# Cutting the stores of one chunk by rows into unequal pieces

## The chip, the cores and the metric

The kernel runs on one core of one Trainium2 chip. The engines are called by their usual names: TensorE, VectorE, ScalarE (ACT), GpSimd and SyncE (SP). The profile counts sixteen DMA engines; here they move data between HBM and the tiles of 128 partitions in the on-chip memory (SBUF). A "row" below is one partition's share of a store: 6 x 1024 floats, 24,576 bytes, for the wide chunks. Every transfer in the traces names a semaphore, and its landing is recorded as updates of that semaphore, called "landing marks" below. Each of the eight stores of chunk 14 left sixteen marks in the trace of before; with sixteen engines in the profile, one mark is read as one engine.

## The reference, cut to what matters

```
emb = emb_table.at[0].set(0.0)            # 100001 x 128
e = emb[seq]                              # 1024 x 50 x 128
uF = cumsum(e, axis=1) / min(t, length)
y = batch_norm(uF)                        # over the 1024 sequences
...                                       # 50 spiking steps: v += (x - v) / 2; spike where v >= 1
uF_out = spikes.mean(axis=0)              # 1024 x 128
scores = uF_out @ emb.T                   # 1024 x 100001 floats: 410 MB
```

The last line is what this case is about: 410 MB must be written.

## The kernel before

The first stage gathers embeddings and runs the 50 steps. The second multiplies the spike counts with the table and stores the scores. Its columns come in chunks, `WIDTHS` giving their width in parts of 1024 columns; each chunk has eight blocks of 128 output rows. A block is collected in one of three buffers `o` and leaves in one store.

```python
WIDTHS = [2, 2, 2, 3, 3, 3, 3] + 12 * [6] + [4, 4]
...
    def store(n, c0, o):
        nc.sync.dma_start(out=out[n * P : (n + 1) * P, c0 : c0 + o.shape[1]], in_=o)
...
    for c, W in enumerate(WIDTHS):
        ...
                turns = [(rowp, "rows2", 6), (rowp, "rows3", 6), (op, "o", 6)]     # c >= 7
        ...
        for n in range(NB):                                                        # NB = 8
            pool, tag, most = turns[blocks % len(turns)]
            o = pool.tile([P, most * HALF], F32, tag=tag, name=f"o_{c}_{n}")
            for q in range(q0, q1):
                ...                                        # products into PSUM, copied to o
            if c or n > 1:
                store(n, q0 * HALF, o[:, : min(N, q1 * HALF) - q0 * HALF])
            ...
            if n in (1, 4) and c >= MIDDLE and to_fetch < parts:
                ...
                fetch(r, to_fetch, GROUP // 2)             # 1.5 MB of table, issued from ACT
```

## Time and profile before

| | before |
|---|---|
| median of the runs | 1576.41 us |
| profiled execution: span | 1646.4 us |
| profiled execution: first store to end | 1064.3 us |
| stores of 3 MB | 96, 20.3 us to landing |
| DMA share and GB/s, 60 us from the start of chunk 14 | 1.00, 416 |

One caution for reading the traces. The stage before the first store takes about 511 us in some executions and about 585 us in others, with the same program. The profiled execution of before is one of the long ones, which is why its span is 70 us above the median.

From the first store on the executions agree: up to chunk 14, where all kernels of this case are alike, the fourteen traces took 638.5 to 639.9 us. So I compare traces by this second stage, and runs only with the runs of before on the same chip in the same rounds.

### The profile page before, as it was taken

The page shows a single profiled execution, that of the slowest core. Times are in us where ns is not written, and L with a number is a line of the kernel's source. Part 1 is how long each engine was busy: PE and PEld are TensorE (multiplying, and loading weights), DVE is VectorE, ACT ScalarE, POOL GpSimd, SP SyncE. Part 2 cuts the span into 40 slices and gives each one's busy share as a digit, 9 for nine tenths or more (in the row PEclk, how much of TensorE's full clock was granted, in tenths as well). Part 3 has the DMA queues.
Part 4 walks back from the last instruction along what each step waited for, and adds up shares of the span by engine and source line. Part 5 has one row for each costly group of instructions (what it writes and reads, how often), then busy time and mean ns, then how long its engine had stood idle before and what let it go on. Part 6 is the DMA issues. An engine that isn't in the chain of part 4 may idle for free.

```text
span 1646.4 us, 12555 instructions
## 1 busy us (share of the span) xinstructions
PE 1115.2 (68%) x4538; PEld 829.4 (50%) x4548; DVE 940.4 (57%) x1161; ACT 630.6 (38%) x700; POOL 379.3 (23%) x406
## 2 busy tenths in 40 slices
PE   4344433444334498889987888888888888788885
PEld 2122211222113276667766666666666666666664
DVE  4566655666556766557655555555555555555553
ACT  2222222222222255446544444444444444444442
POOL 7666666666666500000000000000000000000000
PEclk9999999999755599999999999999999999999998
DMA  9511111111111179999999999999999999999898
GB/s 342 213 45 48 47 48 43 47 48 48 48 43 49 39 320 412 416 422 398 426 422 429 432 428 427 421 420 429 420 423 412 415 421 421 428 425 423 381 428 350
DMA packets 53691, 488.14 MB, mean 296 GB/s; under 512 B 11995, under 2 KB 12796, under 8 KB 32380
## 3 DMA queue, kind: packets, MB, share of 16 engines
q1 hardware_dynamic: 31984, 428.77, 62.0%
q0 software_dynamic: 12800, 26.24, 5.5%
q10 hardware_dynamic: 8844, 32.33, 5.0%
q8 instruction: 36, 0.59, 0.1%
q14 instruction: 27, 0.22, 0.0%
HBM read 77.69 MB, written 409.60 MB: 296 GB/s over the span
## 4 chain that ended last, share of the span: by engine, by line
DMA 48%; DVE 22%; another core or an unknown queue 10%; PE 9%; ACT 5%; issue 4%; POOL 1%; DVEq 0%; ACTq 0%; SPq 0%
DMA scores<-o 48%; PE po L149 8%; ACT o L456 4%; DVE bs L306 4%; DVE uF L305 4%; DVE v L342 3%; DVE s L326 3%; DVE negv L348 3%; DVE o L454 2%; POOL e L187 1%; DVE a L335 1%; DVE mv L316 1%; DVE q L332 0%; PE pt L119 0%
## 5 line engine op out<-in xcount | busy, mean ns | idle before, releaser
L454 DVE TENSOR_SCALAR o<-po 128x1024 f32<-128x1024 f32 x391 | 463.7, 1221 | 352.4 <-DMA scores<-o 326.9
L456 ACT ACTIVATE o<-po 128x1024 f32<-128x1024 f32 (+1 forms) x391 | 388.0, 1019 | 548.2 <-DMA scores<-o 345.0
L187 POOL DMA_INDIRECT e<-in_L_rec_emb_table,idx x400 | 378.6, 947 | 188.8 <-issue 109.8
L149 PE MATMUL po<-pairs,countB 128*128 128x512 f32 x1168 | 313.9, 415 | 66.8 <-ACT o L456 49.6
L149 PEld LDWEIGHTS po<-pairs,countB 128*128 128x128 f32 x1168 | 225.4, 198 | 131.3 <-ACT o L456 64.4
L149 PE MATMUL po<-pairs,countC 128*128 128x512 f32 x876 | 238.2, 417 | 43.2 <-ACT o L456 43.0
L253 PE MATMUL pre<-zT,l 128*128 128x512 f32 x100 | 74.6, 748 | 247.2 <-DVE uF L305 159.5
L149 PEld LDWEIGHTS po<-pairs,countC 128*128 128x128 f32 x876 | 168.8, 199 | 89.3 <-ACT o L456 54.8
L253 PEld LDWEIGHTS pre<-zT,l 128*128 128x128 f32 x100 | 27.7, 279 | 286.9 <-issue 183.0
L305 DVE SCALAR_TENSOR_TENSOR uF<-rlen,pre 128x512 f32<-128x512 f32 x100 | 68.0, 680 | 180.5 <-remote 145.0
L320 ACT ACTIVATE r<-mv,eps 128x1 f32<-128x1 f32 x50 | 14.7, 295 | 378.8 <-DVE mv L316 269.4
L142 DVE TENSOR_TENSOR pairs<-pt,pairs 128x1024 fp32r<-128x1024 f32 (+1 forms) x73 | 88.4, 1217 | 94.7 <-ACT pairs L141 94.7
L296 PE MATMUL pre<-ident,e 128*128 128x128 f32 x400 | 107.2, 426 | 25.8 <-DMA e<-in_L_rec_emb_table,idx 17.7
L119 PE MATMUL pt<-ident,rows 128*128 128x128 f32 x782 | 113.1, 292 | 8.3 <-ACT o L456 3.7
L119 PEld LDWEIGHTS pt<-ident,rows 128*128 128x128 f32 x782 | 102.3, 154 | 28.6 <-issue 9.8
L296 PEld LDWEIGHTS pre<-ident,e 128*128 128x128 f32 x400 | 85.3, 223 | 60.9 <-DMA e<-in_L_rec_emb_table,idx 32.2
L149 PE MATMUL po<-hi,countB 128*128 128x512 f32 x200 | 82.9, 414 | 19.2 <-ACT o L456 14.9
L264 PE MATMUL sums<-s,ident_h 128*128 128x512 bf16 x88 | 45.3, 606 | 64.2 <-DVE s L326 32.8
L149 PE MATMUL po<-lo,countB 128*128 128x512 f32 x200 | 80.4, 402 | 0.0
L149 PE MATMUL po<-pairs,countA 128*128 128x512 f32 (+1 forms) x292 | 73.5, 393 | 9.1 <-ACT o L456 9.1
L141 ACT CAST pairs<-pt 128x1024 fp32r<-128x1024 f32 (+1 forms) x73 | 73.6, 1008 | 15.0 <-PE pt L119 14.9
L149 PE MATMUL po<-hi,countC 128*128 128x512 f32 x150 | 63.2, 421 | 17.7 <-ACT o L456 17.7
(76 smaller groups left out, 849.8 us busy)
## 6 DMA issues: line engine op xcount, KB each, us to landing
scores<-o SPq DMA_DIRECT2D x96, 3072.0 KB, 20.3
scores<-o SPq DMA_DIRECT2D x32, 1536.0 KB, 9.0
rows<-in_L_rec_emb_table ACTq DMA_DIRECT2D x20, 1536.0 KB, 29.2
scores<-o SPq DMA_DIRECT2D x22, 1024.0 KB, 8.6
rows<-in_L_rec_emb_table SPq DMA_DIRECT2D x6, 3072.0 KB, 42.7
scores<-o SPq DMA_DIRECT2D x8, 2048.0 KB, 13.2
scores<-o SPq DMA_DIRECT2D x8, 1872.5 KB, 11.3
e<-in_L_rec_emb_table,idx POOLq DMA_INDIRECT x400
```

The source lines that it names most:

```text
L119: nc.tensor.transpose(pt[:, k0 : k0 + kw], r[:kw, k0 : k0 + D], ident[:kw, :kw])
L141: nc.scalar.copy(vh, vp)
L142: nc.vector.tensor_tensor(vl, vp, vh.bitcast(F32), ALU.subtract)
L149: nc.tensor.matmul(po[:, :kw], lhsT=counts[n], rhs=part[:, k0 : k0 + kw], start=j == 0, stop=j == 1,)
L187: nc.gpsimd.indirect_dma_start(out=es[t][:, n * P : (n + 1) * P], out_offset=None, in_=table, in_offset=bass.IndirectOffsetOnAxis(ap=idx[: ...
L253: nc.tensor.matmul(pre[h], lhsT=l, rhs=zT[:, h * BANK : (h + 1) * BANK], start=t == 0, stop=False, skip_group_check=True,)
L296: nc.tensor.matmul(pre[h][:, k : k + P], lhsT=e[:, h * BANK + k : h * BANK + k + P], rhs=ident, start=False, stop=last, is_transpose=True, ...
L305: nc.vector.scalar_tensor_tensor(uF[:, cs], rlen[:, cs], 1.0 / (t + 1), pre[h], ALU.max, ALU.mult)
L306: nc.vector.bn_stats(bs[:, h, :], uF[:, cs])
L326: nc.vector.tensor_single_scalar(s, v, V_TH, ALU.is_ge)
L454: nc.vector.tensor_scalar_mul(o[:, h0 : h0 + hw], po[:, :hw], 1.0 / T)
L456: nc.scalar.mul(o[:, h0 : h0 + hw], po[:, :hw], 1.0 / T)
```

## The change

It leaves bytes, arithmetic and buffers alone. The eight stores of chunk 14 become transfers of unequal numbers of rows, and two stores of the last chunk become 120 and 8 rows.

```diff
+UNEVEN = 14
+PIECES = [(1, 7, 120), (2, 6, 120), (3, 5, 120), (4, 4, 120), (40, 88), (24, 104), (56, 72), (9, 15, 104)]
...
-    def store(n, c0, o):
-        nc.sync.dma_start(out=out[n * P : (n + 1) * P, c0 : c0 + o.shape[1]], in_=o)
+    def store(n, c0, o, pieces=(P,)):
+        b = 0
+        for rows_of in pieces:
+            nc.sync.dma_start(
+                out=out[n * P + b : n * P + b + rows_of, c0 : c0 + o.shape[1]],
+                in_=o[b : b + rows_of, :],
+            )
+            b += rows_of
+        assert b == P
...
-                store(n, q0 * HALF, o[:, : min(N, q1 * HALF) - q0 * HALF])
+                pieces = (P,)
+                if c == UNEVEN:
+                    pieces = PIECES[n]
+                elif c == len(WIDTHS) - 1 and n % 4 == 3:
+                    pieces = (120, 8)
+                store(n, q0 * HALF, o[:, : min(N, q1 * HALF) - q0 * HALF], pieces)
```

## The prediction

Three things to know for this text and for the expectations:

- "Ports" and "port conflicts" name an assumption: DMA engines that read certain partitions at once hold each other up. "Full step" is its worst case, in which every row concerned takes two row times of 912 ns. The packet records name no engine.
- That one engine is in every piece was assumed too. With 10 + 10 + 10 + 10 + 12 + 10 + 10 + 10 rows it would have 82 where it had 64: 18 more, 16.4 us at 912 ns, an estimate.
- "Eight semaphores in turn" is in the records: in the trace of before the issues of SyncE name eight, 25 or 26 transfers to each if the loads of ScalarE, which use the same ones, are counted too. The store issued at 1548.0 us names the same one as the load issued at 1501.9 us, whose last mark came 46.0 us after issue. The gathers from GpSimd name eight others.

> **What bounds the kernel now.** I read the forty slices first, then the chain of waits, the issues of transfers, and the windows around the stores that change. The slices show two stages. Up to about 580 us the sixteen DMA engines are a tenth busy; from then on they are at 9 tenths in every slice, moving 400 to 430 GB/s, almost to the end:
>
> ```profile
> DMA  9511111111111179999999999999999999999898
> GB/s 342 213 45 48 47 48 43 47 48 48 48 43 49 39 320 412 416 422 398 426 422 429 432 428 427 421 420 429 420 423 412 415 421 421 428 425 423 381 428 350
> ...
> DMA scores<-o 48%; PE po L149 8%; ACT o L456 4%; DVE bs L306 4%; DVE uF L305 4%; DVE v L342 3%; DVE s L326 3%; DVE negv L348 3%; DVE o L454 2%; POOL e L187 1%; DVE a L335 1%; DVE mv L316 1%; DVE q L332 0%; PE pt L119 0%
> ...
> scores<-o SPq DMA_DIRECT2D x96, 3072.0 KB, 20.3
> ```
>
> The chain of waits is stores for 48% of the span. The 96 stores of 3 MB (twelve chunks of eight blocks) land 20.3 us after issue. Chunk 14's eight are issued from 1225.6 to 1288.3 us. The chain in order of time shows the rhythm there, for every third store: about 20 us of landing, about 4 us to refill the freed buffer.
>
> ```profile
> 1251.03 20.67 DMA scores<-o
> 1272.88 2.13 PE po L149 x8
> 1276.09 20.32 DMA scores<-o
> 1297.58 2.13 PE po L149 x8
> 1300.79 20.94 DMA scores<-o
> ```
>
> Three buffers go round, so one store is issued per 25/3 = 8.4 us. When a store is issued the two before it are mostly still queued, so a late issue is cheap. The windows confirm that the engines never lack work there, and show the single place where they do:
>
> ```profile
> 1180.00:1250.00 70.00, 56.91 (x249) 44.42 (x248) 37.01 (x32) 29.41 (x31) 0.00 (x0) 0.94 1.00 418
> 1250.00:1320.00 70.00, 59.93 (x262) 47.67 (x261) 36.78 (x31) 31.67 (x32) 0.00 (x0) 0.92 0.99 417
> ...
> 1540.00:1550.00 10.00, 8.08 (x36) 6.37 (x35) 4.60 (x4) 4.00 (x4) 0.00 (x0) 1.00 0.62 262
> ...
> SPq L158 <- DMA rows<-in_L_rec_emb_table: 13.4, 1, 13.4
> ```
>
> The last two columns of the windows are the DMA share and GB/s; TensorE is busy 60 of 70 us and not the bound. The last line is SyncE's one long wait for a load: transfers of the hardware queues use eight semaphores in turn, and one store had to wait for a slow load that held its semaphore.
>
> Two readings go below the views, to the trace's own records of packets and landings. A 24,576-byte row is one packet, of 912 ns in the median. Each DMA engine leaves its own landing mark, and these show that the sixteen are not equal: of the store issued at 1276.1 us the eighth or ninth engine finishes 12.8 us after issue, the fifteenth 15.1, the last 20.3. **One straggler engine is some 6 us (six to seven rows) behind the rest, and it alone paces the stores.** Its lag grows by about 0.9 us per 35 us after 786 us, which fits the instruction-fetch packets (36 of 16 KB, about 0.95 us each, one per 35 us) all going to it.
>
> [...]the 33-row load left eleven engines' marks. The slowest of these came at 1551.8 us, when only the straggler still had store rows[...].
>
> [...]a 1.5 MB load (24 packets of 4 KB per engine) takes 29.2 us among store rows, and 24 x (0.912 + 0.159) = 26 us.
>
> **The change part by part.** No byte, no arithmetic and no buffer changes. Eight stores become twenty in chunk 14, and two of the last chunk become four.
>
> Issue: fourteen more at 0.332 us, on SyncE, which mostly waits. Nothing on the path.
>
> Engine loads[...], in rows: 128 rows are 8 on each engine, 64 for the chunk. Pieces of 1, 7 and 120 use 1, 7 and 15 engines (1, 1 and 8 rows each); 40 and 88 use 10 and 11 (4 and 8); 24 and 104, 12 and 13 (2 and 8); 56 and 72, 14 and 12 (4 and 6); 9, 15 and 104, 9, 15 and 13 (1, 1 and 8). [...]The part is worth 10 to 17 us.
>
> Last chunk: 120 + 8 rows put 9 rows[...] instead of 8, twice; a row of 14,980 bytes takes 0.57 us, so 1.1 us. **Without port conflicts the sum is 11 to 18 us: about 1590.**
>
> Ports: I assume that a piece is cut into runs of neighbouring partitions[...]. Most engines land within 0.5 us of each other, so they stay in step, [...]I take 40 to 70 us, centre 58. **With port conflicts: about 1635.**
>
> **The rivals.** First, counts alone (1587 to 1595). For it: the profile shows no port conflict[...]. [...]Second, conflicts (1616 to 1652); reversed arguments. Third, the wait moves to SyncE: with two to three transfers per store, eight semaphores cover only three stores, some 25 us, less than the 29 us of a load, so the second piece of the fifth store may wait about 4 us for the load issued after the second. Two stores are queued then, so the engines should not starve: 0 to 4 us. [...]Nothing makes the kernel faster, because the path's engine gains rows in every case I find likely.
>
> **Range and chances.** [...]I give conflicts 58%[...]. The mixture is 0.42 x 1590 + 0.58 x 1635 = 1616. I predict 1618 us, range 1586 to 1652. Slower by over 2% begins at 1607.9, which is past the first outcome and short of the second: 0.57 slower, 0.42 the same, 0.01 faster.
>
> **What would show it.** Look at chunk 14, from about 1225 us. The store records should show 20 issues, with the loss all there and the rhythm before and after unchanged. If counts alone hold, packets of 24,576 bytes stay at 912 ns, DMA share falls to about 64/82 of before, 0.78, in that window, and it grows by 10 to 17 us. If conflicts hold, many packets there take about 1.8 us, the busy share stays high while GB/s falls towards 250 to 300, and the window nearly doubles. A long wait of SyncE for a landing with idle engines would show the third rival.[...]

## More of the kernel before

The metric is device microseconds of one execution; medians are over the fast runs.

The following line, from the view of the tile `scores` of the kernel before, gives the first and the last issue of a store (582.1 and 1634.3 us from the start):

```profile
L158 SPq DMA_DIRECT2D scores<-o x172: 332/332/361, 582.1 to 1634.3; - x172
```

## The result, and the profile after

| | before | after |
|---|---|---|
| median of 4 runs | 1576.41 us | 1634.72 us |
| first store to end, profiled | 1064.3 us | 1121.3 us |
| chunk 14: its first copy into `o` to that of chunk 15 | 67.7 us | 103.3 us |
| from there to the first copy of chunk 20 | 309.7 us | 324.0 us |
| from there to the end | 47.7 us | 55.4 us |

The kernel became 3.7% slower, by 58.3 us: ratio 1.0369, 95% interval 1.0351 to 1.0387. (Ratios are the mean time of one kernel's fast runs over that of the other's in the same rounds, so not quite the ratio of the medians.) The three lower rows are taken from the start times of the copies in the two traces. Up to chunk 14 the two are alike (639.2 and 638.5 us from the first store). Chunk 14 loses 35.6 us until its last block starts to be followed by chunk 15, another 14.3 us shows in the next chunks, mostly while chunk 14's last stores land, and the last chunk loses 7.7 us.

The same line of the tile `scores` after:

```profile
L163 SPq DMA_DIRECT2D scores<-o x187: 236/332/3836, 511.4 to 1617.6; - x187
```

Store number one comes at 511.4 us here, so chunk 14 starts about 1151 us in this trace and about 1222 us in the one of before. The forty slices of the kernel after have a hole there, which those of before have not, in GB/s but hardly in the DMA share:

```profile
DMA  9622222222224999999999999999987899999898
GB/s 341 227 53 52 54 53 52 53 53 53 52 54 187 417 411 421 398 421 425 429 428 431 426 428 413 421 421 428 324 281 211 338 402 422 428 429 425 380 422 297
```

Windows of 60 us from the start of chunk 14 say it in one line each. The columns are the window, its length, busy time with number of instructions for TensorE, its weight loads, VectorE, ScalarE and GpSimd, then granted clock, DMA share and GB/s. First the kernel before, then after:

```profile
1222.00:1282.00 60.00, 47.25 (x209) 37.18 (x210) 30.33 (x27) 26.25 (x28) 0.00 (x0) 0.94 1.00 416
```

```profile
1151.00:1211.00 60.00, 41.83 (x171) 32.82 (x170) 24.68 (x22) 20.81 (x21) 0.00 (x0) 0.86 0.95 298
```

The engines are nearly as busy as before (0.95 against 1.00) and move 298 GB/s where they moved 416. So in this window they are hardly short of work: their packets are slow. The packet records agree. In 120 us from the start of chunk 14, 34% of the 24,576-byte packets take over 1.5 us, in the kernel before 1%; half of all still take up to 949 ns.

The chain of waits of the kernel after, in order of time, has the same rhythm as before until 1136 us, then landings of 29 to 40 us, then the rhythm again:

```profile
1136.43 20.68 DMA scores<-o
...
1163.63 28.93 DMA scores<-o
...
1199.31 30.09 DMA scores<-o
...
1233.09 39.78 DMA scores<-o
...
1278.91 25.20 DMA scores<-o
...
1308.49 20.70 DMA scores<-o
```

And there is a new wait. SyncE waited three times for a load, once for 28.8 us, in the middle of chunk 14 (stores were issued at 1199.3 and next at 1230.6 us); before, it was one wait of 13.4 us, near the end of the program:

```profile
SPq L163 <- DMA rows<-in_L_rec_emb_table: 50.7, 3, 28.8
```

Towards the end of this wait, with nothing issued, the engines do run dry, as two windows of the kernel after show:

```profile
1215.00:1225.00 10.00, 7.93 (x32) 6.32 (x32) 3.58 (x3) 3.98 (x4) 0.00 (x0) 0.66 0.63 210
1225.00:1235.00 10.00, 4.43 (x11) 3.47 (x11) 4.62 (x4) 2.53 (x3) 0.00 (x0) 0.69 0.47 115
```

That makes three suspects: more rows on some engines than on others ("counts"), engines that hold each other up by the partitions they read at once ("conflicts", in the texts on record "ports"), and waiting for a semaphore that a load holds ("semaphores": the store issued at 1230.6 us names the one of the load issued at 1199.4, whose last mark came at 1230.5). The experiments part them.

### The profile page after: what moved, and what is told of

It is laid out like the page before. It is cut to its first block, busy times and chain, and to the rows that moved or that the text cites. A ratio compares the mean times of both kernels' runs of the same rounds, so it can differ in the third digit from the quotient of the medians.

```text
span 1632.6 us, 12593 instructions
## 1 busy us (share of the span) xinstructions
PE 1170.1 (72%) x4548; PEld 834.7 (51%) x4548; DVE 942.1 (58%) x1161; ACT 631.6 (39%) x700; POOL 378.3 (23%) x406
## 4 chain that ended last, share of the span: by engine, by line
DMA 53%; POOL 17%; PE 11%; issue 9%; ACT 5%; DVE 3%; SPq 0%; ACTq 0%; DVEq 0%; POOLq 0%
DMA scores<-o 46%; POOL e L197 17%; PE po L152 10%; ACT o L466 4%; DMA e<-in_L_rec_emb_table,idx 4%; DMA rows<-in_L_rec_emb_table 3%; DVE o L464 2%; PE pt L122 0%; ACT pairs L144 0%; PE pre L306 0%; SPq L163 0%; DVE bs L316 0%; DVE pairs L145 0%; DVE uF L315 0%; DVE s L336 0%
## 5 line engine op out<-in xcount | busy, mean ns | idle before, releaser
L152 PE MATMUL po<-pairs,countB 128*128 128x512 f32 x1168 | 320.6, 421 | 83.9 <-ACT o L466 66.2
L152 PEld LDWEIGHTS po<-pairs,countB 128*128 128x128 f32 x1168 | 230.5, 202 | 150.0 <-ACT o L466 80.9
L152 PE MATMUL po<-pairs,countC 128*128 128x512 f32 x876 | 245.7, 427 | 60.1 <-ACT o L466 59.5
L306 PE MATMUL pre<-ident,e 128*128 128x128 f32 x400 | 155.6, 451 | 150.1 <-DMA e<-in_L_rec_emb_table,idx 148.7
L152 PEld LDWEIGHTS po<-pairs,countC 128*128 128x128 f32 x876 | 174.0, 205 | 107.5 <-ACT o L466 71.3
L306 PEld LDWEIGHTS pre<-ident,e 128*128 128x128 f32 x400 | 79.0, 200 | 245.4 <-DMA e<-in_L_rec_emb_table,idx 223.2
L274 PE MATMUL sums<-s,ident_h 128*128 128x512 bf16 x98 | 49.6, 609 | 61.0 <-DVE s L336 61.0
L349 ACT ACTIVATE v<-uF,hgb,a 128x1024 f32<-128x1024 f32 x49 | 59.2, 1208 | 37.5 <-DVE a L345 37.3
```

The lines of the kernel that those rows point to most:

```text
L152: nc.tensor.matmul(po[:, :kw], lhsT=counts[n], rhs=part[:, k0 : k0 + kw], start=j == 0, stop=j == 1,)
L274: nc.tensor.matmul(sums[h], lhsT=ident_h, rhs=s[:, h * BANK : (h + 1) * BANK], start=t == 0, stop=t == T - 2, skip_group_check=True,)
L306: nc.tensor.matmul(pre[h][:, k : k + P], lhsT=e[:, h * BANK + k : h * BANK + k + P], rhs=ident, start=False, stop=last, is_transpose=True, ...
L349: nc.scalar.activation(vt, uF[:, cs], AF.Identity, bias=hgb[:, 1:2], scale=a)
```

## The experiments

Two jobs landed on other chips, where the kernel before takes 1652.19 and 1648.95 us; in those profiles the stage before the first store takes 583 to 587 us, and the stage of the stores is as long as elsewhere up to chunk 14 (639 to 640 us). The column "loss" is the difference of the two medians of the same rounds. "Slow" is the share of 24,576-byte packets that took over 1.5 us, in 120 us from the start of chunk 14; a shift of that window by 1 us changes it by up to a point.

| run | before | this | loss, us | ratio | slow |
|---|---|---|---|---|---|
| the change | 1576.41 | 1634.72 | 58.3 | 1.0369 | 34% |
| chunk 14 alone | 1652.19 | 1703.05 | 50.9 | 1.0313 | 33% |
| halves, 64 + 64 | 1652.19 | 1690.70 | 38.5 | 1.0241 | 47% |
| cut by columns | 1652.19 | 1653.93 | 1.7 | 1.0012 | 1% |
| the change, loads from GpSimd | 1652.19 | 1708.41 | 56.2 | 1.0333 | 29% |
| before, loads from GpSimd | 1576.27 | 1576.97 | 0.7 | 1.0005 | 0% |
| 18 extra rows on one engine | 1576.27 | 1582.76 | 6.5 | 1.0048 | 1% |
| 120 + 8, eight times | 1576.27 | 1624.61 | 48.3 | 1.0305 | 39% |
| last chunk alone | 1576.27 | 1587.82 | 11.5 | 1.0073 | 1% |
| middle 64 twice (wrong result) | 1648.95 | 1649.86 | 0.9 | 1.0009 | 1% |
| 32 + 64 + 32 | 1648.95 | 1679.48 | 30.5 | 1.0193 | 23% |
| quarters, in order | 1648.95 | 1700.71 | 51.8 | 1.0338 | 56% |
| quarters, alternating | 1648.95 | 1672.28 | 23.3 | 1.0165 | 17% |

The 95% intervals of the ratios mean 1 to 4 us either way, but some 6 us for the change with loads from GpSimd and 7 us for 32 + 64 + 32, whose four runs spread over 12 us. A check from inside: the time from the first store to the end of each profile, less the 1064.3 us of before, agrees with the loss within 2.5 us in every run but the change with loads from GpSimd (61.7 us; its profiled run was the slowest of its four).

The absolute times in the texts on record are meant for a chip with before at 1576; the difference is what to compare.

**Chunk 14 alone.** The last chunk's stores are whole again.

```diff
-                elif c == len(WIDTHS) - 1 and n % 4 == 3:
-                    pieces = (120, 8)
```

> The changed kernel with the pieces of chunk 14 alone; the two stores of the last chunk are whole again. My term for the last chunk was 1.1 us, which would give 1633.6. If those two stores also meet a wait for a semaphore or ports in step, as the 4 to 5 us lost after chunk 14 in the trace suggest, 1629 to 1631. Either way the chunk keeps over 50 us.

The loss is 50.9 us, below the 53 to 57 of the expectation, so by difference (across two chips) the last chunk costs 7.4 us, well over the term of 1.1.

**Halves.** As above, and equal halves in chunk 14.

```diff
-PIECES = [(1, 7, 120), (2, 6, 120), ... (9, 15, 104)]
+PIECES = 8 * [(64, 64)]
```

> Chunk 14's eight stores as 64 and 64 rows: every engine keeps 4 + 4 = 8 rows, so no imbalance[...]. Theory ports: 8 rows take up to 16 row times, 8 x 7.3 us less a lead of 6, so about 1620 to 1635, and most 24,576-byte packets of the chunk take about 1.8 us. Theory counts (only rows per engine matter): 1576 to 1579, packets stay at 912 ns. Theory semaphores (SyncE waits for a load): 16 transfers in the chunk, at most one wait of a few us, 1576 to 1585.

The loss is 38.5 us with a cut that was meant to leave eight rows on every engine, and the engines were busy (0.94 in the window below), so unequal counts are not needed for most of the loss. The window of this run shows the same picture as the change, a high DMA share and few bytes:

```profile
1226.00:1286.00 60.00, 40.40 (x158) 31.70 (x159) 24.15 (x21) 19.40 (x21) 0.00 (x0) 0.86 0.94 274
```

It is below the 44 us that I expected at least, and 47% of the packets are slow, not most; why not more, the runs do not show.

**Cut by columns.** The same number of transfers per block as in the change, each of 128 rows.

```diff
-                store(n, q0 * HALF, o[:, : min(N, q1 * HALF) - q0 * HALF], pieces)
+                many = PIECES[n] if c == UNEVEN else 1      # PIECES = [3, 3, 3, 3, 2, 2, 2, 3]
+                cols = (min(N, q1 * HALF) - q0 * HALF) // many
+                for j in range(many):
+                    store(n, q0 * HALF + j * cols, o[:, j * cols : (j + 1) * cols], pieces)
```

> Chunk 14's stores cut by columns into as many transfers as in the changed kernel (3,3,3,3,2,2,2,3), each of 128 rows: equal engines, [...]only the number of transfers on the eight semaphores is the same. Theory semaphores: SyncE waits 20 us or more for a load again, 1595 to 1610. Theory ports and theory counts: 1576 to 1581; a short wait for a load may show but is hidden by the queue.

The loss is 1.7 us. SyncE waits for loads here too, three times and 38.9 us together, but the longest is 13.9 us and the engines keep their speed. (The 1% in the table counts neighbouring chunks only, since the packets of chunk 14 are smaller here; these too are quick, 312 ns in the median for 8,192 bytes and 460 for 12,288.)

```profile
SPq L163 <- DMA rows<-in_L_rec_emb_table: 38.9, 3, 13.9
```

```profile
1227.00:1287.00 60.00, 48.59 (x202) 38.23 (x202) 29.75 (x25) 25.42 (x26) 0.00 (x0) 0.89 0.99 409
```

The number of transfers as such costs next to nothing.

**Loads from GpSimd, in the change and in the kernel before.** By the records of before, transfers issued from GpSimd name semaphores that no store names (eight against eight others), so no store should have to wait for a load.

```diff
-        engine = nc.sync if q < AHEAD * GROUP else nc.scalar
+        engine = nc.sync if q < AHEAD * GROUP else nc.gpsimd
```

> The changed kernel with the later table loads issued from GpSimd, whose transfers use other semaphores, so that no store can wait for a load by sharing one. Theory ports: the 28.8 us wait of SyncE vanishes, but the engines were mostly busy with slow packets during it, so 5 to 20 us come back: 1612 to 1630. Theory semaphores: nearly all comes back: 1585 to 1600. Theory counts: 1590 to 1600.

> The kernel before with the later table loads issued from GpSimd: the base for the run with the changed kernel's loads moved, which was 56 us over the kernel before although the wait of SyncE had gone. If moving the loads costs nothing by itself, 0 to -4 us against the kernel before, and the 28.8 us wait was worth nothing. If it costs 10 us or more, the wait was worth that much after all.

In the changed kernel SyncE no longer waits for any load, and the loss is still 56.2 us. In the kernel before the move costs 0.7 us. By the medians the 28.8 us wait was worth 58.3 - (56.2 - 0.7) = 2.8 us, a difference across two chips and smaller than its noise. The traces are sharper: from the first copy of chunk 14 to that of chunk 20, the change lost 49.9 us against before, and with the loads moved in both kernels it lost 51.2. The wait cost nothing there. I had expected 5 to 20 us back: a miss. The wait looks terrible in the view of waits and in the windows, yet it lies beside engines that were late anyway: the 88-row piece issued just before it, at 1199.3 us, left its last mark at 1229.4, one us before the wait ended. While some engines ran dry (DMA share 0.63 and 0.47), others still worked off rows of that piece: three of its marks came 29.1 to 30.1 us after issue.

**18 extra rows on one engine.** The kernel before, with 18 one-row stores of partition 0 to a scratch tensor among the stores of chunk 14.

```diff
+EXTRA = [2, 2, 2, 2, 4, 2, 2, 2]
+                if c == UNEVEN:
+                    for j in range(EXTRA[n]):
+                        nc.sync.dma_start(out=scratch[sum(EXTRA[:n]) + j : sum(EXTRA[:n]) + j + 1, :], in_=o[0:1, :])
```

> The kernel before with 18 extra one-row stores of partition 0 to a scratch tensor among chunk 14's stores (2, 2, 2, 2, 4, 2, 2, 2): one engine gets exactly the 18 rows[...]. Theory counts as I predicted it: 10 us if that engine leads the straggler by 6 us, 16.6 us if it is the straggler; packets stay at 912 ns. Theory ports alone: 0 to 3 us.

6.5 us, where 18 rows take 18 x 0.912 = 16.4 us: if one engine carries them all, as assumed, about 10 us of them vanish in its lead over the straggler. The packets keep their 912 ns; the DMA share falls instead (0.86), which fits engines that wait for one. This is what counts alone look like, and it is not what the changed kernel shows:

```profile
1151.00:1211.00 60.00, 45.41 (x208) 35.84 (x208) 28.68 (x25) 24.59 (x25) 0.00 (x0) 0.95 0.86 357
```

**120 + 8, eight times.**

```diff
+PIECES = 8 * [(120, 8)]
```

> All eight stores of chunk 14 as 120 and 8 rows. By counts only one row more[...] per store: 8 rows, 7.4 us less a lead of 6, so 1 to 8 us. [...]Anything from 30 to 60 is for ports.

48.3 us, for conflicts, with 39% of the packets slow. This one cut brings nearly the loss of the eight different cuts of the change (50.9).

**The last chunk alone.**

```diff
-                if c == UNEVEN:
-                    pieces = PIECES[n]
-                elif c == len(WIDTHS) - 1 and n % 4 == 3:
+                if c == len(WIDTHS) - 1 and n % 4 == 3:
                     pieces = (120, 8)
```

> The last chunk's two stores as 120 and 8 rows and nothing else. My term was 1.1 us (one row of 0.57 us, twice). The trace of the changed kernel and the run without this part put it at 7 to 8 us. Theory ports: 2 x 8 extra row times of 0.57 us = 9.1 us in full step, so 6 to 9. Theory counts: 1 to 2.

11.5 us, more than the 6 to 9 I expected from conflicts and ten times the term of the prediction. The packets of 14,980 bytes, which only this chunk has, average 682 ns instead of 572, and about one in eight takes over 1.1 us. My expectation, 9.1 us at most, was an estimate from eight extra row times of 0.57 us in each of two stores, and too low. The last chunk of the traces loses 11.3 us here, 11.4 in the change with loads from GpSimd and 7.7 in the change itself, so 7.4 and 11.5 are two cases and not noise. What goes with it is the straggler: in that chunk's whole stores before the first cut, its mark came 3.5 to 6.6 us after the fifteenth in the first two traces, and 0.5 to 0.7 us in the third. Why that should cost more is not shown.

**Middle 64 twice.** Here the theory of conflicts is tried alone: the same two transfers of 64 rows to the same rows of the output as in the halves, but both read partitions 32 to 95. Its output is wrong, which doesn't matter for the time.

```diff
-                in_=o[b : b + rows_of, :],
+                in_=o[b : b + rows_of, :] if len(pieces) == 1 else o[32:96, :],
```

> Chunk 14 as 64 and 64 rows as in the halves, same transfers, same rows of the output, but both halves read partitions 32 to 95 of the tile. [...]The result is wrong on purpose. Theory ports: back to 0 to 3 us over the kernel before, packets at 912 ns. If the halves' 38 us came from anything else (the number of transfers, the rows written together, 64-row transfers as such), it stays at 30 to 40 us.

0.9 us, against 38.5 us for the halves, although SyncE waited for loads here too (47.0 us together, the longest 18.7). Only the source partitions differ, so the loss is a matter of which partitions are read at once, not of 64-row transfers, of the rows written, or of the number of transfers.

```profile
1223.00:1283.00 60.00, 49.55 (x215) 39.18 (x214) 30.88 (x27) 27.00 (x28) 0.00 (x0) 0.91 0.95 395
```

**32 + 64 + 32.** A correct result with the good middle.

```diff
+PIECES = 8 * [(32, 64, 32)]
```

> Chunk 14 as 32, 64 and 32 rows, a correct result[...]. Theory ports: the outer 64 rows of each store take 4 extra row times in full step, half of what the halves lose, so about 15 to 25 us. Anything else but ports: as the halves or more, 35 to 45, since there are more transfers.

30.5 us, above my 15 to 25. Four extra row times per block, if each row of the outer pieces takes two (an estimate), are 8 x 4 x 0.912 = 29.2 us, less a lead of 6 us 23. So this cut, which has a good middle, lost more than that sum allows (31.2 us by its trace too), though less than the 35 to 45 for "anything else". Either the lead is not to be taken off where the straggler's own rows are slow as well, or the pieces of a block also hold each other up; the runs don't tell which.

**Quarters in two orders.** The same four transfers of 32 rows, once with starts 0, 32, 64, 96, once with 0, 64, 32, 96.

```diff
+PIECES = 8 * [(0, 32, 64, 96)]      # starts of 32 rows each; the other run: (0, 64, 32, 96)
```

> Chunk 14 as four times 32 rows in order 0, 32, 64, 96[...]. As the halves by ports: 30 to 50 us. If the number of transfers mattered, clearly more than the halves.

> The same quarters in order 0, 64, 32, 96[...]. If two engines[...] stay strictly in step, the order is nothing and it loses as much as the other order, up to 55 us. If engines drift[...] it loses clearly less: 5 to 25 us.

51.8 us in order, a little above my 30 to 50, and 23.3 us alternating, inside my 5 to 25. In order, the packets took about 1.65 us in the median, a quarter of them over 1.9, where whole stores have 912 ns. Eight extra row times for each of eight blocks, an estimate from two row times per row, are 64 x 0.912 = 58.4 us, less a lead of 6 us 52.4: near full step, if the lead is rightly taken off (see the run above). Alternating, more than half of that goes away, and slow packets fall from 56% to 17%. The first 60 us of chunk 14, in order and then alternating:

```profile
1222.00:1282.00 60.00, 38.77 (x153) 30.38 (x151) 21.50 (x18) 17.88 (x18) 0.00 (x0) 0.84 0.88 247
```

```profile
1223.00:1283.00 60.00, 43.73 (x176) 34.56 (x175) 25.48 (x22) 21.75 (x22) 0.00 (x0) 0.86 0.92 309
```

The order alone is what was changed; why it matters was not shown, since the records don't name engines.

## Why the prediction was right

The measured 1634.7 us lies in the range (1586 to 1652), slower by over 2% was given 0.57, and the outcome called "with port conflicts: about 1635" is what happened. That the median fell within 1 us of 1635 is partly luck, as the terms show. Point by point:

- **The bound.** The stores bound the kernel before and after; the loss sits where their stage changed, and 639 us of that stage ahead of it are the same.
- **How many engines, and which.** In the trace after, the first three pieces of 1, 7 and 120 rows left 1, 7 and 15 landing marks (besides one early mark of each), and every other piece of chunk 14 left as many as the prediction's count of its engines: 10 and 11 for 40 and 88 rows, 12 and 13 for 24 and 104, 14 and 12 for 56 and 72, 9, 15 and 13 for 9, 15 and 104. So the number of engines holds; which engines they are, the marks can't show. The seven-row piece's last mark came 15.3 us after issue, the others by 8.7, and the one-row piece's at 6.8. So the straggler is probably one of the seven engines of that piece and not the engine of the one-row piece. That the engine with most rows led it was an assumption; the run with 18 rows fits it (6.5 us of 16.4).
- **Issues.** Miscounted: chunk 14 has twenty-one transfers, not twenty, and the program fifteen more issues, not fourteen (187 against 172 above). "Nothing on the path" is nearly so: a few issues took longer than 0.332 us, up to 3.8, and two of them, 1.8 and 1.6 us, stand in the chain of waits in chunk 14.
- **Counts.** Predicted at 10 us for a leading engine; the 18 rows alone measured 6.5. Right in kind, a little too large: if one engine had them all, the lead was worth 10 us, not 6. The marks that the prediction quotes allow that: 6 us is about the distance to the slower of the other engines (20.3 - 15.1 = 5.2), while the eighth is 20.3 - 12.8 = 7.5 us ahead. And the straggler's lag grows only up to about 1024 us; from then to chunk 14 and through it, it stays at 4.4 to 6.2 us over the fifteenth.
- **Conflicts.** The step that decided the case. It rested on an assumption; that the partitions read at once decide is borne out by the middle 64 against the halves: 0.9 and 38.5 us. What the engines then share, the traces don't show. The size, 40 to 70 us with a centre of 58, was the author's estimate; the chunk lost 50.9. The premise that most engines land within 0.5 us of each other was too strict: in chunk 14's stores before, the first nine marks already spread over 0.1 to 1.5 us. The order of pieces, which the estimate did not have, is worth 28.5 us in the quarters (51.8 against 23.3).
- **The last chunk.** This term was mis-sized: 1.1 us predicted, 7.4 (by difference) to 11.5 us (alone) measured. I had counted rows there and left out the conflicts, although it is the same cut of 120 rows. So two errors cancel in the total: the chunk 7 us under its centre of 58, the last chunk 6 over its term.
- **The wait of SyncE.** Predicted as a rival at about 4 us of wait and 0 to 4 us of cost. The wait was 28.8 us: two loads of chunk 14 landed 38.9 and 31.1 us after issue, where the median before is 29.2, beside rows of which a third took over 1.5 us, and the store waited for the second of these loads. That the engines should not starve was wrong too (shares of 0.63 and 0.47). The cost stayed in the predicted range of 0 to 4 us: none is seen in the traces.
- **The signs.** High DMA share, GB/s at 298 and slow packets came as foretold (a quarter of the packets took over 1.73 us); "many packets" meant a third, and the window grew by half (67.7 to 103.3 us), not to double.

What stays open: how counts (6.5 us), conflicts and the order of the pieces share the 50.9 us of the mixed chunk, since they don't add up simply; why 32 + 64 + 32 lost more than its sum allows; and why the last chunk costs 7.4 us in one case and 11.5 in another.

## What to carry to other kernels

When a store-bound stage has one transfer of 128 partitions per block, leave it in one piece, or cut it by columns (1.7 us here); the cuts by rows here changed how many landing marks a transfer leaves (1 to 15 for sixteen in chunk 14), which partitions are read together, or both, and the second cost far more (38.5 us for equal halves, against 6.5 us for 18 rows more on one engine). If a cut by rows must be, let pieces of the lower and the upper 64 partitions alternate: that was the cheapest correct cut by rows tried here (23.3 us). A good middle of partitions 32 to 95 cost next to nothing by itself (0.9 us), but with the outer rows, which must leave too, it was 30.5. A long wait of the issuing engine proves nothing until it has been taken away: 28.8 us of it cost nothing that the traces show.
